# Pool memsets between the indirect transfers of some side chains in a four-layer kernel

## The chip, the cores and the metric

The kernel runs on one core of a Trainium2 chip. The metric is the device time of one execution in microseconds, as the median of several executions without the profiler. Besides these, one execution was taken by the hardware profiler; all durations of single instructions come from it.

## What is computed

Four layers follow each other on x of 4 x 1024 tokens with 128 features, all in float32. Each layer is an attention-like part and a feed-forward part, each added to x and followed by a layer norm:

```python
x = L0_attn_x                                                # (4, 1024, 128)
x = _layernorm(x + _L0_attn_ref(x, ...), axis=-1)            # scans along the tokens
x = _layernorm(x + _L0_ffn_ref(x, ...), axis=-1)             # quantised product
x = _layernorm(x + _L1_attn_ref(x, ...), axis=-1)            # complex linear recurrence
x = _layernorm(x + _L1_ffn_ref(x, ...), axis=-1)             # 16 experts, 4 per token, and a shared one
x = _layernorm(x + _L2_attn_ref(x, ...), axis=-1)            # causal softmax attention, 16 heads of 8
x = _layernorm(x + _L2_ffn_ref(x, ...), axis=-1)             # 8 experts, 2 per token
x = _layernorm(x + _L3_attn_ref(x, ...), axis=-1)            # gated Toeplitz mix over the batch rows
x = _layernorm(x + _L3_ffn_ref(x, ...), axis=-1)             # 32 experts, 4 per token, and a shared one
```

The feed-forward parts of layers 1 to 3 are what matters here. In each, a router gives every token its k best experts and their weights. The token's output is the weighted sum of what these experts make of it, for instance in layer 3:

```python
topk_scores, topk_idx = jax.lax.top_k(softmax(flat @ router_w.T + router_bias), 4)
h = silu(einsum('nd,ehd->neh', flat, gate_w)) * einsum('nd,ehd->neh', flat, up_w)
expert_out = einsum('neh,edh->ned', h, down_w)
out = (take_along_axis(expert_out, topk_idx[:, :, None], axis=1) * topk_scores[:, :, None]).sum(1)
```

## The kernel before

**Tiling.** x stays in SBUF as 32 tiles of 128 tokens by 128 features. Tiles are grouped in four quarters of the sequence, and the layers work on parts: in layer 1 part a (quarters 0 and 1) and part r (quarters 2 and 3), in layer 2 a, m and n (m and n are quarters 2 and 3 of two batch rows each), in layer 3 a, b and c (b and c are one quarter each).

**The expert stage, as five steps.** A route function (l1_route, l2_route, l3_route, each ending in positions) runs mostly on DVE. It computes for every token and choice a row in a list sorted by expert: the tiles pos, for instance posl1r for layer 1, part r, written at L1276. spread (L1313) scatters the tiles of x into that list in DRAM (l1rr, l2ra, l2rm, l2rn, l3ra, l3rb, l3rc), with one indirect transfer for each tile and choice, 128 rows of 512 bytes. The experts function (small_experts for layers 1 and 3, l2_experts for layer 2) loads the list in groups of 512 rows (xg) and computes each tile with its expert's weights. Each such load waits for all transfers of the list. It writes the result to another list (l1yr, l2ya, ...). collect (L1381) gathers the rows of each tile back (yt), again with one indirect transfer for each tile and choice, and DVE adds them, weighted, to x (L1392). Then the tiles are normed and the next layer begins.

All indirect transfers go through one helper, indirect (L1299, the transfer itself at L1301), on Pool's queue. The helper also ties every transfer behind the two before it, so that they stay in the order of the program.

**The order of the work.** The functions are generators. Each yields an estimate, in microseconds, of what the step just emitted will take. run drains a generator; mix(main, side) emits the main generator's steps, and after each as many of the side generator's steps as the estimates allow (pace is a factor on the side's), so that the side's instructions stand between the main's on PE, ACT, DVE and Pool. queued adds that a side instruction stands behind the last main one of its engine. With drain, the rest of the side comes after the main; press drains the side until a condition holds. served lets a chain be served together with others that begin once a condition holds, and chain and abreast put generators one behind the other or side by side. One indirect transfer is entered as 1.26 us, at three places: spread and collect yield 1.26 times the choices, and indirect adds 1.26 to moved_by, the date by which Pool is thought to have issued all so far. collect adds a tile's rows no earlier than moved_by + 4.0 in planned time.

**The stages that the change touches**, in the order of the method all:

| main stage | side beside it |
|---|---|
| l2_attn(0): layer 2 attention, quarters 0 and 1 | l1_route(r), spread of l1rr |
| l1_experts(r), l1_shared(r) | loads of wall2, l2_route(a), spread of l2ra |
| l2_experts(a2) | l1_close(r): collect of l1yr, norm, transposes |
| l2_attn(1): layer 2 attention, quarters 2 and 3 | collect of l2ya, l3_attn(a), l3_route(a), spread of l3ra; once enough rows are done, route and spread of l2rm and l2rn |
| l2_experts(m2), l2_experts(n2) | the rest of these; collect of l2ym |
| l3_shared(a), l3_experts(a) | collect of l2yn, l3_attn(b), l3_route(b) |
| l3_shared(b), l3_experts(b), then the same for c | spread of l3rb and l3rc, collect of part a and b, l3_attn(c), l3_route(c) |

l3_shared(b) and (c) put their result in a tile of its own, which DVE adds to x (L1962) when the scatter of that part has read x.

Of the kernel before, what the change touches and what calls it, by code (L numbers as in the profile page):

```python
# [20 lines left out]
P = 128  # L21
B, L, D = 4, 1024, 128
# [18 lines left out]
E1, F1, NG1, TKG1, K1 = 16, 128, 4, 2, 4  # L41
# [2 lines left out]
FS3 = 512  # L44

H3, D13 = 8, 256

RND = 12582912.0
PI_IN = 3.1415925
# [25 lines left out]
class Kernel:  # L75
    def __init__(self, ctx, tc, ins, out, cols, consts, rows):
        self.tc, self.nc, self.ins, self.out = tc, tc.nc, ins, out
        self.count = itertools.count()
        nc = self.nc
        self.const = self.pool(ctx, "const")  # L80
        self.small = self.pool(ctx, "small", 3)
        self.routes = self.pool(ctx, "routes")
        self.side = self.pool(ctx, "side", 2, space=PSUM)
        dram = self.pool(ctx, "dram", space=DRAM)

        self.cols_t = self.load(self.const, ins["cols"])
        self.cst_t = self.load(self.const, ins["consts"])
        self.x = self.tile(self.const, [P, NT, D], "x")
        self.xT = self.tile(self.const, [P, NT * P], "xT")
        nrow = ins["rows"].shape[1]  # L90
        self.rows_t = self.tile(self.const, [P, nrow], "rows")
        nc.gpsimd.dma_start(out=self.rows_t, in_=ins["rows"].to_broadcast([P, nrow]))
        self.col = {k: self.cols_t[:, a:b] for k, (a, b) in cols.items()}
        self.cst = {k: self.cst_t[:, a:b] for k, (a, b) in consts.items()}
        self.row = {k: self.rows_t[:, a:b] for k, (a, b) in rows.items()}
        self.ident = self.cst["ident"]
        self.eps = self.tile(self.const, [P, 1], "eps")
        nc.vector.memset(self.eps, LN_EPS)
        self.halfpi = self.tile(self.const, [P, 1], "halfpi")
        nc.vector.memset(self.halfpi, math.pi / 2)  # L100
        self.ones = self.tile(self.const, [P, E3], "ones")
        nc.vector.memset(self.ones, 1.0)
        self.rnd = self.tile(self.const, [P, 1], "rnd")
        nc.vector.memset(self.rnd, RND)
        self.zero = self.tile(self.const, [P, D], "zero")
        nc.gpsimd.memset(self.zero, 0.0)
        self.flag = self.tile(self.const, [1, 1], "flag", I32)
        self.hm = self.tile(self.const, [P, 4], "hmg")

        self.first, self.rest = Part("a", 0, 2), (Part("b", 2, 1), Part("c", 3, 1))  # L110
        self.parts = (self.first, *self.rest)
        self.by_rows = (
            Part("a", 0, 2, range(B), 0), Part("m", 2, 2, (0, 1), NT // 2), Part("n", 2, 2, (2, 3), 3 * NT // 4)
        )

        self.rows_done = 0

        self.listed = set()

        self.traced, self.latest = nc.cur_bb.bb.instructions, {}  # L120
        self.now = self.moved_by = 0.0
        self.moved = []

        self.lists, self.route = {}, {}
        self.both = (self.first, Part("r", 2, 2))
        for lay, ne, k in (("l1", E1, K1), ("l2", E2, K2), ("l3", E3, K3)):
            for pt in {"l1": self.both, "l2": self.by_rows, "l3": self.parts}[lay]:
                tl = -(-((pt.nt * P * k + (P - 1) * ne) // P) // 4) * 4
                self.lists[lay, pt.name] = (
                    self.tile(dram, [tl * P, D], f"{lay}r{pt.name}"), self.tile(dram, [tl * P, D], f"{lay}y{pt.name}"), tl  # L130
                )
        self.wall2 = self.tile(dram, [P, E2 * 3 * F2], "wall2")
        self.xsave = self.tile(dram, [P, NT, D], "xsave")

        self.ksave = self.tile(dram, [P, B, BLK], "ksave")
        self.vsave = self.tile(dram, [P, B, 4, (NH + 1) * VW], "vsave")
# [1162 lines left out]
    def indirect(self, apart=(), **kw):  # L1299

        ins = self.nc.gpsimd.indirect_dma_start(**kw)  # L1301

        for o in apart:
            self.tc.declare_no_dep(ins.ins, o.ins.name, reason="rows differ")
        behind = mybir.DependencyInfo(mybir.DependencyClass.NoSync, mybir.DependencyReason.DATA)
        mine = [o.ins.name for o in apart]
        for o in [o for o in self.moved if o not in mine][-2:]:
            self.tc.add_manual_dep(ins.ins, o, behind, reason="queued behind")
        self.moved = self.moved[-130:] + [ins.ins.name]
        self.moved_by = max(self.moved_by, self.now) + 1.26  # L1310
        return ins

    def spread(self, lay, part, k):  # L1313

        pos, _, _, done, _ = self.route[lay + part.name]
        rows = self.lists[lay, part.name][0]
        for t in range(part.nt):
            for i in range(k):
                ins = self.indirect(
                    apart=done,  # L1320
                    out=rows, out_offset=bass.IndirectOffsetOnAxis(ap=pos[:, t, i : i + 1], axis=0),
                    in_=self.x[:, part.order[t], :], in_offset=None,
                )
                done.append(ins)
            yield (1.26 * k,)
        self.listed.add(lay + part.name)

    def gathered(self, pool, rows, g, done, want):
# [52 lines left out]
    def collect(self, lay, part, k, yp, first=0, nt=None, which=None):  # L1381

        nc = self.nc
        pos, wk = self.route[lay + part.name][:2]
        assert f"made {lay}{part.name}" in self.listed
        ys = self.lists[lay, part.name][1]
        late = []

        def add():
            t, yt, _ = late.pop(0)  # L1390
            for i in range(k):
                nc.vector.scalar_tensor_tensor(  # L1392
                    self.x[:, part.order[t], :], yt[:, i, :], wk[:, t, i : i + 1], self.x[:, part.order[t], :],
                    ALU.mult, ALU.add,
                )

        for t in which or range(first, first + (nt or part.nt)):
            yt = self.tile(yp, [P, k, D], "yt")
            for i in range(k):
                self.indirect(  # L1400
                    out=yt[:, i, :], out_offset=None, in_=ys,
                    in_offset=bass.IndirectOffsetOnAxis(ap=pos[:, t, i : i + 1], axis=0),
                )

            late.append((t, yt, self.moved_by + 4.0))
            if len(late) == yp.bufs:
                while late[0][2] > self.now:
                    yield (1.0,)
                add()
            yield (1.26 * k,)  # L1410
        while late:
            while late[0][2] > self.now:
                yield (1.0,)
            add()
            yield (0.36 * k,)
# [471 lines left out]
    def all(self):  # L1887
        a, rest = self.first, self.rest
        b, c = rest
        r = self.both[1]  # L1890
        a2, m2, n2 = self.by_rows
        with ExitStack() as ctx:
            lgp = self.pool(ctx, "l2lg")
            self.l2_lg = self.tile(lgp, [P, NT, E2], "lg")
            with ExitStack() as early:
# [13 lines left out]
                with ExitStack() as c2:  # L1909
                    wall = self.l1_wall(c2)  # L1910
# [3 lines left out]
                    self.run(self.mix(self.abreast(self.l2_weights(), side), self.l1_close(a, yp)))  # L1914
            with ExitStack() as c2:
                wall = self.l1_wall(c2)
                self.run(self.mix(self.l2_attn(0), self.chain(self.l1_route(r), self.spread("l1", r, K1))))
                wall2, loads = self.l2_wall(c2, True)
                yp = self.pool(c2, "l1yr", 5, right=True)
                self.run(self.mix(self.chain(self.l1_experts(r, wall), self.l1_shared(r)), self.chain(loads, self.routed(a2))))  # L1920
                self.run(self.mix(self.l2_experts(a2, wall2), self.l1_close(r, yp)))
            listed = lambda name: lambda: name in self.listed
            on = self.served(
                self.chain(self.rows_in(a2), self.onward(a, True)),
                (lambda: self.rows_done >= B + 2, self.routed(m2)),
                (lambda: self.rows_done == 2 * B, self.routed(n2)),
            )
            self.run(self.mix(self.l2_attn(1), on, drain=False))
            with ExitStack() as c3:
                with ExitStack() as c2:  # L1930
                    wall = self.l2_wall(c2)
                    self.press(on, listed("l2m"))
                    self.run(self.mix(self.l2_experts(m2, wall), on, drain=False))
                    self.press(on, lambda: {"l2n", "routed l3a"} <= self.listed)
                    sw, wall3 = self.l3_wall(c3, True)
                    on = self.chain(on, self.rows_in(m2))
                    self.run(self.mix(self.l2_experts(n2, wall), on, drain=False))
                self.press(on, listed("l3a"))
                yp = self.pool(c3, "l3y", 8)
# [207 lines left out]
```

## Time and profile before

| what | value |
|---|---|
| median of 3 executions without the profiler | 2050.22 us (2046.76 to 2051.03) |
| the profiled execution | 2413.21 us |
| its span, first to last instruction | 2411.4 us |
| mean granted clock of TensorE in it | 0.818 |
| PE busy (matmul) | 1616.9 us, 67% of the span |
| DVE busy | 1263.6 us, 52% |
| ACT busy | 825.0 us, 34% |
| Pool busy | 722.6 us, 30%, of which nearly all indirect transfers |

The profiled execution took 363 us longer than the median of the others. A group in the profile is one line of the code with its operation and tiles; it is given with its count, its busy time, the mean duration of one in nanoseconds, and the time for which its engine sat idle just before, with what ended that. PE is the matmul, PEld the load of its weights. "issue" stands for idle time in which the engine waited for nothing that the profile shows, "remote" for a wait whose end the profile can't put down to an instruction. For Pool's indirect transfers the busy time is that on Pool; the data land later.

The streams of transfers that the change touches, in the profiled execution:

| stream | transfers | first start to last end, us |
|---|---|---|
| l1rr | 64 | 703.3 to 784.2 |
| l2ra | 32 | 957.5 to 997.8 |
| yt from l1yr | 64 | 1024.3 to 1182.7 |
| yt from l2ya | 32 | 1214.7 to 1294.0 |
| l2rm | 16 | 1488.7 to 1508.7 |
| l2rn | 16 | 1653.1 to 1673.0 |
| l3ra | 64 | 1722.5 to 1810.7 |
| yt from l2ym | 16 | 1811.0 to 1830.8 |

### The profile page before, as it was taken

What the parts mean: (1) busy time and instruction counts of PE and PEld (TensorE: products, weight loads), DVE (VectorE), ACT (ScalarE), POOL (GpSimd) and SP (SyncE); (2) the same over time, 40 slices, a digit from 0 to 9 for tenths busy, and PEclk for the clock granted to TensorE, in tenths of its full rate; (3) what the DMA queues carried; (4) which work ended last, traced back from release to release, by engine and by line L of the source; (5) the groups of instructions that cost most, each with busy time, mean ns of one, the idle gap of its engine ahead of it and who ended that gap; (6) DMA issues with size and microseconds to landing.
All of it is one profiled execution on the core that took longest, in us unless ns stands there. A gap on an engine that the chain in (4) does not pass through costs nothing. (4 is left out here: it accounts for less than half of the span.)

```text
span 2411.4 us, 27036 instructions
## 1 busy us (share of the span) xinstructions
PE 1616.9 (67%) x9017; PEld 967.3 (40%) x9017; DVE 1263.6 (52%) x3630; ACT 825.0 (34%) x1180; POOL 722.6 (30%) x681
## 2 busy tenths in 40 slices
PE   7626876975661778487969787887745798357160
PEld 3214333853320337345623232344523486245160
DVE  8957894655570565224545675473611265236233
ACT  6701571422330333122236564642201164223030
POOL 1031484135227000435132002002272200735725
PEclk9856887988785888788979998988977899678575
DMA  9930002334101016212130000031321131222232
GB/s 309 288 112 0 20 34 90 112 115 160 62 31 53 15 34 200 83 44 74 38 106 21 1 1 16 3 114 40 143 85 35 44 112 46 76 79 62 89 89 68
DMA packets 215530, 187.10 MB, mean 78 GB/s; under 512 B 16528, under 2 KB 194064, under 8 KB 214864
## 3 DMA queue, kind: packets, MB, share of 16 engines
q1 hardware_dynamic: 194672, 142.29, 18.7%
q0 software_dynamic: 20704, 42.86, 5.8%
q8 instruction: 84, 1.38, 0.2%
q14 instruction: 70, 0.57, 0.1%
HBM read 88.49 MB, written 96.60 MB: 77 GB/s over the span
## 5 line engine op out<-in xcount | busy, mean ns | idle before, releaser
L1055 ACT ACTIVATE pr<-sc 128x1024 f32<-128x1024 f32 x288 | 279.7, 1021 | 319.9 <-PE sc L157 184.9
L157 PE MATMUL gu<-ld,xgT 128*128 x640 | 177.4, 423 | 88.8 <-issue 38.7
L157 PE MATMUL sc<-qm,kT 32*128 32x512 f32 (+3 forms) x1536 | 199.2, 558 | 13.7 <-issue 12.3
L157 PE MATMUL s<-pr,va 128*32 128x512 f32 (+3 forms) x1536 | 177.1, 528 | 46.0 <-issue 26.2
L157 PEld LDWEIGHTS gu<-ld,xgT 128*128 128x128 f32 x640 | 127.5, 210 | 119.1 <-issue 49.7
L165 PE MATMUL tp<-ld,hg 128*128 128x128 f32 x624 | 104.0, 289 | 92.1 <-ACT hT L167 38.0
L169 DVE COPY hT<-tp 128x512 f32<-128x512 f32 x118 | 81.0, 686 | 159.3 <-remote 73.9
L157 PE MATMUL gu<-wall,xgT 128*128 x304 | 156.1, 640 | 2.7 <-ACT xgT L167 2.0
L1061 DVE TENSOR_TENSOR pr<-pr,ld 128x512 f32<-128x512 f32 (+1 forms) x160 | 92.2, 581 | 100.6 <-ACT pr L1055 98.5
L165 PEld LDWEIGHTS tp<-ld,hg 128*128 128x128 f32 x624 | 81.5, 149 | 144.7 <-issue 46.9
L165 PE MATMUL tp<-ld,xg 128*128 128x128 f32 x396 | 68.9, 305 | 102.1 <-DMA xg<-l3rc 48.5
L1749 DVE TENSOR_TENSOR hg<-sg,gu 128x256 f32<-128x256 f32 x160 | 65.8, 417 | 134.9 <-ACT sg L1748 95.8
L167 ACT COPY xgT<-tp 128x512 f32<-128x512 f32 x99 | 58.0, 586 | 213.0 <-PE tp L165 91.1
L157 PEld LDWEIGHTS sc<-qm,kT 32*128 32x128 f32 x1536 | 84.8, 197 | 113.6 <-issue 77.4
L1507 ACT ACTIVATE sg<-gu 128x512 f32<-128x512 f32 x76 | 45.2, 597 | 225.7 <-PE gu L157 109.4
L1748 ACT ACTIVATE sg<-gu 128x256 f32<-128x256 f32 x160 | 61.1, 385 | 163.2 <-PE gu L157 80.9
L1301 POOL DMA_INDIRECT l1ra<-x,posl1a x64 | 93.1, 1455 | 59.5 <-DVE posl1a L1276 40.3
L157 PEld LDWEIGHTS s<-pr,va 128*32 128x32 f32 x1536 | 38.9, 113 | 156.6 <-issue 109.5
L1509 DVE TENSOR_TENSOR hg<-sg,gu 128x512 f32<-128x512 f32 x76 | 51.7, 682 | 92.1 <-ACT sg L1507 48.7
L1301 POOL DMA_INDIRECT yt<-l1yr,posl1r x64 | 60.9, 951 | 124.1 <-DVE x L1392 79.3
L165 PEld LDWEIGHTS tp<-ld,xg 128*128 128x128 f32 x396 | 52.4, 158 | 107.6 <-issue 59.0
L1301 POOL DMA_INDIRECT l1rr<-x,posl1r x64 | 61.7, 965 | 99.5 <-DVE posl1r L1276 80.3
(440 smaller groups left out, 3498.8 us busy)
## 6 DMA issues: line engine op xcount, KB each, us to landing
wall<-wall SPq DMA_DIRECT2D x16, 768.0 KB
l3ra<-zero SPq DMA_DIRECT2D x1, 6144.0 KB
ld<-in_l_w SPq DMA_DIRECT2D x2, 3072.0 KB
wall<-we SPq DMA_DIRECT2D x24, 256.0 KB
ld<-in_l_w SPq DMA_DIRECT2D x1, 6144.0 KB
l1ra<-zero SPq DMA_DIRECT2D x1, 5120.0 KB
l1rr<-zero SPq DMA_DIRECT2D x1, 5120.0 KB
xg<-l3ra SPq DMA_DIRECT2D x20, 256.0 KB
```

What stands on the lines that cost most here:

```text
L157: return self.nc.tensor.matmul(out, lhsT, rhs, start=start, stop=stop)
L165: nc.tensor.transpose(pt[:, k * P : (k + 1) * P], s, self.ident)
L167: nc.scalar.copy(dst, pt[:, : n * P])
L169: nc.vector.tensor_copy(dst, pt[:, : n * P])
L1055: nc.scalar.activation(pr, sc[h], AF.Exp)
L1061: nc.vector.tensor_tensor(d, d, cst["tril"].unsqueeze(1).unsqueeze(1).to_broadcast([P, 2, n, P]), ALU.mult)
L1301: ins = self.nc.gpsimd.indirect_dma_start(**kw)
L1507: nc.scalar.activation(sg, gu[:, 0, :], AF.Silu)
L1509: nc.vector.tensor_tensor(h, sg, gu[:, 1, :], ALU.mult)
L1748: nc.scalar.activation(sg, pg[:, :, 0, :], AF.Silu)
L1749: nc.vector.tensor_tensor(h[:, 2 * c : 2 * c + 2, :], sg, pg[:, :, 1, :], ALU.mult)
```

## The change

A new tile idle of 384 columns is only ever written. While a generator is wrapped in spaced, every indirect transfer that it issues is followed on Pool by a memset of 384 (LONG) or 256 (SHORT) columns of that tile, tied behind it. The estimate of one transfer becomes 1.26 us plus 0.0009 us for each column, at the three places that had 1.26. Eight streams are wrapped, the ones of the table above, with SHORT for l3ra and l2ym and LONG for the others. The remaining streams (part a of layer 1, l2yn, and all of layer 3 but l3ra) are as they were.

```diff
+LONG, SHORT = 384, 256
...
+        self.idle = self.tile(self.const, [P, LONG], "idle")
+        self.rest_cols = 0
...
         self.moved = self.moved[-130:] + [ins.ins.name]
-        self.moved_by = max(self.moved_by, self.now) + 1.26
+        if self.rest_cols:
+            stay = self.nc.gpsimd.memset(self.idle[:, : self.rest_cols], 0.0)
+            self.tc.add_manual_dep(stay.ins, ins.ins.name, behind, reason="queued behind")
+            self.moved.append(stay.ins.name)
+        self.moved_by = max(self.moved_by, self.now) + self.step
         return ins
+
+    @property
+    def step(self):
+        return 1.26 + self.rest_cols * 0.0009
+
+    def spaced(self, gen, cols=LONG):
+
+        while True:
+            self.rest_cols = cols
+            got = next(gen, None)
+            self.rest_cols = 0
+            if got is None:
+                return
+            yield got
...
-            yield (1.26 * k,)
+            yield (self.step * k,)
...
-                self.run(self.mix(self.l2_attn(0), self.chain(self.l1_route(r), self.spread("l1", r, K1))))
+                self.run(self.mix(self.l2_attn(0), self.chain(self.l1_route(r), self.spaced(self.spread("l1", r, K1)))))
...
-                self.run(self.mix(self.chain(self.l1_experts(r, wall), self.l1_shared(r)), self.chain(loads, self.routed(a2))))
-                self.run(self.mix(self.l2_experts(a2, wall2), self.l1_close(r, yp)))
+                self.run(self.mix(self.chain(self.l1_experts(r, wall), self.l1_shared(r)), self.chain(loads, self.spaced(self.routed(a2)))))
+                self.run(self.mix(self.l2_experts(a2, wall2), self.spaced(self.l1_close(r, yp))))
...
-                self.chain(self.rows_in(a2), self.onward(a, True)),
-                (lambda: self.rows_done >= B + 2, self.routed(m2)),
-                (lambda: self.rows_done == 2 * B, self.routed(n2)),
+                self.chain(self.spaced(self.rows_in(a2)), self.spaced(self.onward(a, True), SHORT)),
+                (lambda: self.rows_done >= B + 2, self.spaced(self.routed(m2))),
+                (lambda: self.rows_done == 2 * B, self.spaced(self.routed(n2))),
...
-                    on = self.chain(on, self.rows_in(m2))
+                    on = self.chain(on, self.spaced(self.rows_in(m2), SHORT))
```

More of the change, by code (lines that the diff above doesn't have):

```diff
@@ L1409, in collect @@
                 add()
-            yield (1.26 * k,)
+            yield (self.step * k,)
         while late:
```

## The prediction

> **What bounds the kernel now.** I read the page first, then the Pool's groups, then the stretches around each stream of indirect transfers. A stream here is a run of such transfers one behind the other.
>
> ```profile
> span 2411.4 us, 27036 instructions
> ...
> POOL 1031484135227000435132002002272200735725
> ```
>
> The second line is Pool's busy share in 40 slices of 60.3 us: it is no bound, but is full during its streams. Their price, and that of a memset:
>
> ```profile
> L1301 POOL DMA_INDIRECT l1ra<-x,posl1a x64 | 93.1, 1455 | 59.5 <-DVE posl1a L1276 40.3 <-issue 19.2
> ...
> L1301 POOL DMA_INDIRECT l1rr<-x,posl1r x64 | 61.7, 965 | 99.5 <-DVE posl1r L1276 80.3 <-issue 19.2
> ...
> L340 POOL MEMSET keep<- 128x1024 f32 x1 | 1.0, 952 | 0.0
> ...
> L106 POOL MEMSET zero<- 128x128 f32 x1 | 0.2, 232 | 0.0
> ```
>
> Columns: busy us, mean ns of one | idle us before. A transfer holds Pool 0.965 us and is followed by 0.30 us of "issue" (19.2/64): one per 1.265 us. Now what the other engines do beside the 64 transfers of l1rr (703.3 to 784.2 us), columns PE, PEld, DVE, ACT, POOL busy, then PE's clock, DMA share, GB/s:
>
> ```profile
> 632.00:719.00 87.00, 66.68 (x488) 31.68 (x487) 61.68 (x226) 34.51 (x36) 12.09 (x13) 0.87 0.08 30
> 719.00:793.00 74.00, 8.95 (x21) 2.39 (x20) 2.05 (x6) 1.38 (x2) 49.66 (x52) 0.50 0.12 47
> 793.00:900.00 107.00, 87.80 (x763) 43.82 (x763) 68.00 (x175) 45.61 (x47) 0.00 (x0) 0.90 0.05 19
> ```
>
> From 16 us into the stream until 9 us after it, the attention stands still. At the end of the l3ra and l2ym streams (1722 to 1831 us), PE and then ACT:
>
> ```profile
> 1796.29 2.72 PE L157 MATMUL gu<-wall,xgT 128*128 x4
> 1836.97 1.11 PE L165 MATMUL tp<-ld,hg 128*128 128x128 f32 x4 [37.95 <-ACT hT L167]
> ```
>
> ```profile
> 1826.53 0.60 ACT L1507 ACTIVATE sg<-gu 128x512 f32<-128x512 f32 x1 [42.80 <-remote]
> ```
>
> PE's product ends at 1799.0, and ACT, which needs only that, is released at 1826.5: PE's signal is 27.5 us late. I went through every wait of ACT and DVE (over 0.3 us) on PE's semaphore and compared its end with PE's last matmul end before it. With at most 7 indirect transfers begun in the 20 us before: 629 waits, those over 1 us late sum to 4.3 us. With 8 or more: 177 waits, 498 us. Laid on one time line (two engines often wait together), all late stretches cover 250 us, of which 170 beside streams that the change spaces.
>
> So the question is whether executions without the profiler have this hold-up. I think not, for three reasons. The profiled execution took 2413.2 us, 363 more than the median of 2050.2; taking out the 250 us, and 34 us in which PE stutters between two of them (734 to 768), leaves 2129, still above the median. Signals are prompt for the first 10 to 15 us of a stream, and then stop, sooner where PE issues many instructions; the stream beside the light PE work at 505 to 527 us shows at most 3 us. [...] And it is not instructions that are missing: the instruction queue fetched 16 KB in 1.1 us at 743.3, mid-stream.
>
> What bounds the unrecorded kernel is then its stages in turn: PE (67% of the span, 113 of 130 us in the second half of l2_attn(1)) and the hand-over between side chains and stages, as where DVE adds the shared part (columns: us, times, longest):
>
> ```profile
> DVE x L1962 <- DMA l3rc<-x,posl3c: 33.7, 1, 33.7
> ```
>
> [...]
>
> **The change part by part.**
>
> *Memsets.* 224 of 384 columns (64 l1rr, 32 l2ra, 64 l1yr, 32 l2ya, 16 l2rm, 16 l2rn) and 80 of 256 (64 l3ra, 16 l2ym). From the two rows: (952 − 232)/896 = 0.80 ns a column, so 232 + 256 × 0.80 = 437 ns and 335 ns. Pool gets 224 × 0.437 + 80 × 0.335 = 125 us more. Least: they vanish in the 0.30 us of issue but for 0.14 us, 31 + 3 = 34 us; most: each brings an issue of 0.30 of its own, 216 us. I take 1.70 us a transfer (LONG) and 1.60 (SHORT), the earliest memsets on the page standing with no idle time before them. Each waits only for the memset before it on the same engine, so only transfers queue behind it.
>
> *l1rr:* 64 × 0.437 = +28 us: ends at 812. l2_attn(0), which ends at 900, would end at 826 without the 74 us: hidden, 14 us left. At the upper price it ends at 832, 6 us on the path. *l2ra:* +14 us on an end at 86 us after the experts' start at 911; experts and l1_shared last 155, or 124 less hold-up: hidden. *l1yr:* Pool starts 20 transfers before the stage and sits idle 79.3 us of it for DVE's adds (its group's idle time by releaser, x L1392): hidden by that. *l2ya, l2rm, l2rn:* +14, +7, +7 beside l2_attn(1) and l2_experts(m2), whose lists are ready early: hidden; l2rn has the least cover.
>
> *The planner.* The step grows from 1.26 to 1.61 and 1.49, so side work is placed later among PE's, DVE's and ACT's instructions. Built, both kernels have the same instructions on these engines, and the same order on DVE until the first add of l1yr. Three moves stand on the path:
> 1. The norm closing l1_close(r) (L209, 2.1 us, ahead of the last expert tiles now, 1205 us) goes behind the first instructions of l2_attn(1), which needs its transposes: its 2.1 us plus transposes and copies, +4 us (0 to 8).
> 2. l3ra and l2ym: 64 × 0.335 + 16 × 0.335 = +27 us on Pool, and the planner knows 0.23 of the 0.335. Without hold-up, l2ym would be gathered at about 1811 to 1831, ahead of its adds (L1392, after the second block of l3_shared). Afterwards 1836 to 1862, while the adds move by about one block of 10.5 us (1901.6 to 1912.0): DVE waits, with the products of l3_shared behind it and PE behind these. +7 us (0 to 14).
> 3. That lateness shifts l3_attn(b) and l3_route(b). topk and weigh of b (2019.7 to 2024.5, 4.9 us) now lie before the first product of l3_shared(b); afterwards behind four, and the positions behind eight. posl3b comes at 2046.1; I take +7 us (3 to 12). The scatter l3rb follows it with nothing beside it from 2066 to 2089, so this is paid in full.
>
> Of moved steps, each takes its DMAs along: the load of xg waits for all of its list, and SP's other loads queue behind that wait, covered as above. [...]
>
> **Sum:** 4 + 7 + 7 + 2 = +20 us on 2050.2: **2070 us**. Durations come from the profiled execution, whose own sum is another: 2413 + 20 less what spacing frees of the 170 to 204 us of hold-up, about 2250, with the median not following. Main case's own range: 2055 (lower ends, 3 us and more) to 2105 (8 + 14 + 12 + 5 + 6 for l1rr, and as much again unseen).
>
> **The rivals.**
> - *The hold-up is real* and exists unrecorded (the other side). Place: PE's signals beside long streams; price: up to 204 us; it decides as soon as more than 20/204, a tenth, of it remains in plain executions. For it: it begins at a rate, with no hold-up at up to 7 transfers in 20 us, and l1ra at 1.76 us a transfer passes freely (PE 88.8 of 126 us); spacing makes 1.70. Against it: the 363 us. At a third: 2050 + 20 − 68 = 2002 us.
> - *All is hidden*: the waits in 2 and 3 are covered by side work that had slack anyway: 2050 ± 4. For it: l3_attn(b) has the whole of l3_experts(a) to catch up in; against it: scatter l3rb is exposed.
> - *The memset does not space* (it lies within the 0.30 us): only the planner acts: 4 + 7 + 2 = 2063. It belongs with the main case.
>
> **How the numbers follow.** Within 0.2% (4 us) is about what a measurement can tell from no change. Main case with the last rival 0.55, hidden 0.12, real hold-up 0.33: slower 0.55, same 0.12, faster 0.33. The range reaches to the real hold-up at two fifths (2050 + 20 − 82 = 1988) and up to 2105; outside lie about 0.1 below and 0.07 above.
>
> **What would show it.** Step by step in the profile after: transfers 1.70 and 1.60 us apart; l1rr ending before l2_attn(0); a later gap before x L1962 at l3b; waits of DVE at L1392 for l2ym. The late PE signals shrink in the recorded span, by far more than the median does. I am wrong if the median falls with the span.

## The result and the profile after

The change makes the kernel slower: 2104.05 us (2099.95 to 2106.48, 4 runs) against 2050.62 us (2046.76 to 2052.37, 4 runs) beside it, a ratio of 1.0261 with a 95% interval of 1.0239 to 1.0283. That is 53 us more, where 20 were forecast.

The profiled execution of the changed kernel took 2104.62 us, as long as its other executions. The one of the kernel before, from which the prediction was made, had taken 2413.21 us, 363 more than its median. So a difference of these two traces isn't the effect of the change. On the page of after, the line of Pool and the groups that answer to those shown of before are these:

```profile
span 2102.8 us, 27331 instructions
...
POOL 2013078304630880587344000402268700665755
...
L1315 POOL MEMSET idle<- 128x384 f32 (+1 forms) x304 | 124.7, 410 | 0.2
...
L1305 POOL DMA_INDIRECT l1rr<-x,posl1r x64 | 65.1, 1017 | 93.1 <-DVE posl1r L1280 82.5
```

The memsets cost what was worked out (410 ns in the mean; by form 439 ns for 384 columns and 329 ns for 256). But they don't lengthen each transfer by that much: the idle time behind a transfer of l1rr falls from 0.30 us to (93.1 − 82.5)/64 = 0.17 us. Part of a memset lies where Pool waited anyway.

A later run of the kernel before (e12 below) has a trace of an execution as fast as the others: 2049.42 us, beside a median of 2051.87. Its page:

```profile
span 2047.6 us, 27036 instructions
...
POOL 2012168403650570274332000300347600755755
```

**Where the time went.** The next two fences give stretches of this trace and of the trace after, cut at the same points of the program: from DVE's first work for l2_experts(a2), to its last for it, to its last for l2_attn(1), to its last for the experts of m2 and n2, to its first for l3_experts(a). Columns: stretch, length, busy us (count) of PE, PEld, DVE, ACT and Pool, then PE's clock, DMA share and GB/s. First the kernel before (e12), then the changed kernel:

```profile
916.00:1031.00 115.00, 113.60 (x618) 77.66 (x616) 70.97 (x182) 43.15 (x72) 45.30 (x48) 1.00 0.23 70
1031.00:1404.00 373.00, 316.73 (x2391) 123.62 (x2392) 233.96 (x713) 212.83 (x225) 47.57 (x48) 0.94 0.10 33
1404.00:1565.00 161.00, 148.81 (x739) 101.26 (x738) 88.66 (x284) 44.22 (x75) 60.47 (x63) 0.91 0.32 116
1565.00:1620.00 55.00, 47.09 (x205) 29.44 (x206) 17.92 (x36) 10.89 (x19) 41.87 (x44) 0.95 0.26 82
```

```profile
924.00:1052.00 128.00, 116.22 (x611) 78.54 (x609) 69.85 (x172) 39.40 (x67) 79.69 (x116) 0.96 0.23 64
1052.00:1422.00 370.00, 314.92 (x2371) 119.72 (x2372) 223.62 (x672) 215.59 (x229) 67.82 (x96) 0.94 0.09 32
1422.00:1586.00 164.00, 149.51 (x767) 102.06 (x765) 98.86 (x335) 46.89 (x77) 63.90 (x95) 0.93 0.32 114
1586.00:1665.00 79.00, 49.05 (x204) 30.68 (x205) 17.38 (x34) 10.72 (x18) 68.92 (x104) 0.80 0.20 63
```

Two stretches grow, with PE's work in them nearly unchanged: the experts of a2 by 13 us, l3_shared(a) by 24 us. Together with what lies ahead and behind, this is the lateness at each point, in us (times in the trace; the middle column is a run with the memsets alone, e13 below):

| point | before (e12) | memsets alone (e13) | change |
|---|---|---|---|
| Pool's first transfer of l1rr | 678.1 | +2.2 | +7.1 |
| DVE's last of l2_attn(0) | 795.7 | +9.2 | +11.7 |
| DVE's first of l2_experts(a2) | 915.6 | +5.6 | +8.2 |
| ACT's first exponential of l2_attn(1) | 1052.9 | +7.1 | +17.1 |
| DVE's last of l2_attn(1) | 1404.4 | +8.9 | +17.5 |
| DVE's last of the experts of m2 and n2 | 1564.6 | +8.3 | +21.3 |
| DVE's first of l3_experts(a) | 1620.2 | +19.4 | +45.4 |
| DVE's first of l3_experts(b) | 1788.6 | +19.4 | +54.5 |
| end | 2047.6 | +23.4 | +55.2 |

Up to the first transfer of l1rr no memset has run, and PE, DVE and ACT have the same instructions in the same order in all three traces. So the 2.2 and 7.1 us at that point belong to the executions compared, not to the change, and differences of this size between traces of different comparisons can't be read as its effect. In the run with memsets alone the order on these three engines is that of the kernel before to the end.

The waits name the two places. DVE's waits for gathered rows (columns: us, times, longest) in the kernel before (e12), and then in the changed one:

```profile
DVE x L1392 <- DMA yt<-l2ym,posl2m: 5.3, 3, 2.3
```

```profile
DVE x L1414 <- DMA yt<-l2ym,posl2m: 28.6, 2, 27.8
...
DVE x L1414 <- DMA yt<-l1yr,posl1r: 19.2, 8, 9.4
```

At x L1414 (L1392 before) DVE adds the rows of l2ym. It came 27.8 us too early, and PE sat behind it: 49 us of work in 79 us. For l1yr there were no waits at this line before; now 19.2 us, within l2_experts(a2).

**The late signals of PE.** In e12 they aren't there: over 347 waits of DVE and ACT for PE with 8 or more transfers in the 20 us before, the lateness over 1 us sums to 4.6 us, where the trace of 2413 us had 498 over 177. The comparisons below come in two kinds, by the chip on which they ran: the kernel before takes about 2050 us in all its executions (2042.90 to 2062.02), or about 2400 us in all (2387.73 to 2419.24). Only runs beside 2050 us are of the kind in which the change was measured.

### The profile page after: what moved, and what is told of

The parts are those of the page before. It is cut to its first block, busy times and chain, and to the rows that moved or that the text cites. A ratio compares the mean times of both kernels' runs of the same rounds, so it can differ in the third digit from the quotient of the medians.

```text
span 2102.8 us, 27331 instructions
## 1 busy us (share of the span) xinstructions
PE 1547.9 (74%) x9017; PEld 938.8 (45%) x9017; DVE 1265.4 (60%) x3630; ACT 826.6 (39%) x1181; POOL 850.0 (40%) x985
## 5 line engine op out<-in xcount | busy, mean ns | idle before, releaser
L161 PE MATMUL sc<-qm,kT 32*128 32x512 f32 (+3 forms) x1536 | 189.5, 545 | 1.0 <-ACT pr L1059 1.0
L161 PE MATMUL gu<-ld,xgT 128*128 x640 | 169.8, 410 | 23.1 <-DVE hg L1771 20.5
L161 PE MATMUL s<-pr,va 128*32 128x512 f32 (+3 forms) x1536 | 164.2, 523 | 19.2 <-DVE pr L1065 7.7
L161 PE MATMUL gu<-wall,xgT 128*128 x304 | 148.1, 611 | 6.6 <-ACT xgT L171 3.8
L169 PE MATMUL tp<-ld,xg 128*128 128x128 f32 x396 | 65.9, 295 | 88.1 <-DMA xg<-l3rc 49.6
L1315 POOL MEMSET idle<- 128x384 f32 (+1 forms) x304 | 124.7, 410 | 0.2
L1305 POOL DMA_INDIRECT l1ra<-x,posl1a x64 | 93.1, 1454 | 59.3 <-DVE posl1a L1280 40.1
L173 DVE COPY hT<-tp 128x512 f32<-128x512 f32 x118 | 80.7, 684 | 58.4 <-PE tp L169 58.3
L1305 POOL DMA_INDIRECT l1rr<-x,posl1r x64 | 65.1, 1017 | 93.1 <-DVE posl1r L1280 82.5
L169 PE MATMUL tp<-ld,hg 128*128 128x128 f32 x624 | 97.5, 277 | 5.4 <-DVE hg L1771 2.7
L1305 POOL DMA_INDIRECT l2rm<-x,posl2m x16 | 16.1, 1008 | 190.3 <-DVE posl2m L1280 187.8
L1305 POOL DMA_INDIRECT l3ra<-x,posl3a x64 | 63.2, 988 | 66.1 <-DVE posl3a L1280 51.6
```

The lines of the kernel that those rows point to most:

```text
L161: return self.nc.tensor.matmul(out, lhsT, rhs, start=start, stop=stop)
L169: nc.tensor.transpose(pt[:, k * P : (k + 1) * P], s, self.ident)
L173: nc.vector.tensor_copy(dst, pt[:, : n * P])
L1315: stay = self.nc.gpsimd.memset(self.idle[:, : self.rest_cols], 0.0)
```

## The experiments

### The first comparison, beside 2399 us

**e1** is the kernel before, without an edit. 

> The kernel before, unchanged, with a new profile. If PE's late signals are an artefact of one recorded execution, the new profile need not have them: its own time would then lie at 2046 to 2055 us, and shows where the 53 us of the change come from, stage by stage. If they belong to the kernel whenever it is recorded, the profile takes about 2413 us again. If they belong to the kernel as such, no execution is possible at 2050 us without them, and the new profile at 2050 us must show late signals of some tens of us.

It took 2395.95 us, beside 2399.15 us; the profiled execution 2402.8 us. The late signals are in it, in the same places and of the same size (473 us over 172 waits). The reading "an accident of one recorded execution" falls. DVE and ACT wait for releases that the profile can't place:

```profile
ACT pr L1055 <- remote: 117.3, 6, 69.7
ACT sg L1507 <- remote: 65.7, 4, 42.1
DVE hT L169 <- remote: 65.4, 7, 19.0
DVE t L169 <- remote: 62.5, 1, 62.5
```

"remote" waits sum to 538 us here (46 of them, counting groups of 4.8 us and more), and in e12, of the same program, there are none down to groups of 2.5 us. Landings of transfers are fewer on record too: 7951 in this trace, 15601 in that of e12.

**e2**, the planner's step without the memsets:

```diff
-            stay = self.nc.gpsimd.memset(self.idle[:, : self.rest_cols], 0.0)
-            self.tc.add_manual_dep(stay.ins, ins.ins.name, behind, reason="queued behind")
-            self.moved.append(stay.ins.name)
```

> The planner's step of 1.26 + 0.0009 us a column stays, but no memset is emitted: the order of the change with transfers as close as before. Theory (the transfers of l3ra and l2ym end later than the adds that need them): without memsets the gather of l2ym ends 27 us earlier, its wait at the adds goes, and what is left is the norm of l1_close behind the first instructions of l2_attn(1) and the later routing of part b: 2055 to 2070 us. Rival (the order alone costs it): 2095 to 2110 us. Rival (it is only Pool's length): 2046 to 2054 us.

**e3**, the memsets without the planner's step:

```diff
-        return 1.26 + self.rest_cols * 0.0009
+        return 1.26
```

> All 304 memsets are emitted, but the planner's step stays 1.26 us, so the order on PE, DVE and ACT is that of the kernel before (but for steps that wait for the true date). Theory: the gather of l2ym is as late as with the change, and the adds stand where they stood before, so DVE waits for them as long or longer: 2085 to 2110 us, with 25 to 40 us of waiting at the first add of l2ym's rows. Rival (the order alone costs it): 2046 to 2056 us.

**e4**, neither memsets nor step for l3ra and l2ym:

```diff
-                self.chain(self.spaced(self.rows_in(a2)), self.spaced(self.onward(a, True), SHORT)),
+                self.chain(self.spaced(self.rows_in(a2)), self.onward(a, True)),
...
-                    on = self.chain(on, self.spaced(self.rows_in(m2), SHORT))
+                    on = self.chain(on, self.rows_in(m2))
```

> Only the LONG streams are spaced; l3ra and l2ym go as in the kernel before. Theory: the 27.8 us wait of DVE for l2ym's rows goes, and with it the lateness of everything behind it; what is left is the norm of l1_close (4 us, 0 to 8), [...] and whatever the later routing of part b costs: 2052 to 2066 us. Rival (the long spacings cost it, in l2_attn(0) to l2_attn(1)): 2085 to 2105 us.

Measured: e2 2409.24 us, e3 2151.57, e4 2236.83, all beside 2399.15. None of the three fits its expectation, since these were made for a kernel before of 2050 us. The comparison tells something else. In this comparison the time falls with the number of streams that are spaced: e2, which spaces none, stays 10 us above the kernel before, e4, which leaves out l3ra and l2ym, is 162 us below it, and e3, which spaces all eight, 248. In e3 almost no late signal lies beside the streams that it spaces (of its 121 us, 100 lie beside the two gathers of l3ya and l3yb, which it doesn't space). And e3 is faster than the change itself turns out to be here (e5), though both have the same memsets: a first sign that the planner's part costs.

In the traces of e1 and e2 the order can be read, though not the time: l3ra begins 107 us after DVE's last of l2_attn(1) in e1 and 129 us after it in e2, 22 us later with no memset anywhere.

**e5** is the changed kernel, without an edit. 

> The changed kernel, unchanged. In the last comparison the kernel before took 2399 us in every execution, with PE's late signals in its trace, where it had taken 2050 us in the comparison of the change. Theory (late signals are a condition of the chip or of its recording, and spacing takes them away): the changed kernel takes 2095 to 2115 us whatever the kernel before takes beside it, 2050 or 2399 us. Rival (the changed kernel gets slower too under that condition): 2200 us or more beside 2399 us.

It took 2184.32 us beside 2397.67 us: a ratio of 0.9108 (0.9078 to 0.9137). So the change is 9% faster on such a chip and 2.6% slower on the other kind. Theory and rival both miss, and the rival by less: the changed kernel gets slower too, by 80 us. Late signals remain beside the streams that it leaves alone, above all those of layer 3 (late stretches of 99 us in all, with 20 us of DVE's wait for l2ym among them).

**e6** spaces every stream:

```diff
-        self.rest_cols = 0
+        self.rest_cols = LONG
...
-            self.rest_cols = 0
+            self.rest_cols = LONG
             if got is None:
```

> Every stream of indirect transfers is spaced by 384 columns, those of layer 1 part a, l2yn and layer 3 too. Theory (late signals of PE come only with dense streams): none is left in the trace, so the time is the same whether the kernel before takes 2050 or 2399 us beside it: 2104 us plus what the added memsets cost where the stream is waited for, 0.437 us for each of the 32 transfers of l3rb, of l3rc and of the last gather, 42 us, and up to 30 us for the others: 2145 to 2180 us. Rival (late signals come from the volume of records, not their density): with 2399 us for the kernel before, 2220 us or more.

2175.42 us, beside 2407.2: within the theory's range. Hardly a late signal is left: over 371 waits with 8 or more transfers before them the lateness sums to 32 us, and the longest, 15 us, lies at l3_shared(a), where DVE waits for l2ym. Yet landings are missing here too (12271 on record). So signals aren't late wherever records are missing; in these traces they are late where records are missing and the transfers follow each other closely (those of l1rr are 1.26 us apart in e1, with 473 us of lateness in the whole trace, and 1.62 us in e6, with 32).

### The quiet base, beside 2054.6 us

To be free of the chip, all four kernels of this comparison have memsets of 256 columns also behind the transfers that the change leaves alone, not entered with the planner (e7):

```diff
+LONG, SHORT, OTHER = 384, 256, 256
+TOLD = {384: 384, 256: 256}
...
-            self.rest_cols = cols
+            self.rest_cols, self.told = cols, TOLD[cols] if tell else 0
             got = next(gen, None)
-            self.rest_cols = 0
+            self.rest_cols, self.told = OTHER, 0
...
-        return 1.26 + self.rest_cols * 0.0009
+        return 1.26 + self.told * 0.0009
```

> The changed kernel, with 256-column memsets also behind the transfers that the change leaves alone (those are not entered with the planner), so that no stream is dense enough for late PE signals: a common base for the three runs beside it. Expected 2120 to 2155 us: 2104 us, and 0.19 us for each of the 96 transfers of l3rb, l3rc and the last gather, 18 us, and up to 30 us for the others.

**e8** has the same memsets, and the step back at 1.26 (`return 1.26`). 

> All memsets of e7, but the planner's step is 1.26 us everywhere, so the order on PE, DVE and ACT is that of the kernel before. Theory (the longer step pushes DVE's routing of layer 3 part a back by the planned time of the streams before it, 64 x 0.35 = 22 us, and what needs posl3a with it): 15 to 30 us under e7, l3ra begins 15 to 26 us sooner after the end of the second half of layer 2's attention, and DVE's wait for l2ym's rows falls from about 28 to under 12 us. Rival (the memsets' own time on Pool is the whole cost): within 6 us of e7.

**e9** leaves only three chains untold:

```diff
-                self.chain(self.spaced(self.rows_in(a2)), self.spaced(self.onward(a, True), SHORT)),
-                (lambda: self.rows_done >= B + 2, self.spaced(self.routed(m2))),
-                (lambda: self.rows_done == 2 * B, self.spaced(self.routed(n2))),
+                self.chain(self.spaced(self.rows_in(a2), tell=False), self.spaced(self.onward(a, True), SHORT)),
+                (lambda: self.rows_done >= B + 2, self.spaced(self.routed(m2), tell=False)),
+                (lambda: self.rows_done == 2 * B, self.spaced(self.routed(n2), tell=False)),
```

> e7, but the planner isn't told of the memsets of three chains alone: the gather of l2ya and the scatters l2rm and l2rn, which stand beside the second half of layer 2's attention ahead of the routing of layer 3 part a. Theory: these 64 entries of 0.35 us are what pushes l3_route(a) back; l3ra begins 15 to 26 us sooner than in e7, and the time is 10 to 25 us under e7. Rival (the norm of l1_close pushed into the attention, or the entries of l3ra and l2ym, cost it): within 5 us of e7.

**e11** is e8 with the memsets behind l3ra and l2ym doubled:

```diff
+            self.times = 2 if cols == SHORT else 1
...
+            for _ in range(self.times):
                 stay = self.nc.gpsimd.memset(self.idle[:, : self.rest_cols], 0.0)
```

> e8 with two memsets of 256 columns instead of one behind each of the 80 transfers of l3ra and l2ym: about 0.33 x 80 = 26 us more of Pool in that chain. Theory (that chain has little slack left in the old order, 10 us of waiting in the run with memsets alone): 15 to 27 us over e8. Rival (the chain is covered by l3_shared and the experts of n2): within 5 us of e8.

| run | us | against | DVE's wait for l2ym, us (longest) | l3ra begins after DVE's last of l2_attn(1), us |
|---|---|---|---|---|
| e7 change | 2131.38 | | 28.3 (27.7) | 113.6 |
| e8 old order | 2093.86 | e7 − 37.5 | 16.6 (13.2) | 90.9 |
| e9 three chains untold | 2110.5 | e7 − 20.9 | 13.4 (12.8) | 93.9 |
| e11 old order, twice the short ones | 2118.73 | e8 + 24.9 | 40.4 (34.0) | 94.0 |

This comparison fell beside 2054.6 us. The order alone is worth 37.5 us, 20.9 of them in the three chains: telling the planner of 64 transfers more by 384 × 0.0009 = 0.35 us each, 22 us, puts l3_route(a) behind them 20 us later, though it runs on DVE and isn't waiting for them: it needs nothing of the 32 scatters, and the rows of the 32 gathers of l2ya have all been fetched 380 us before it starts (1131.6 and 1512.0 us in the trace after). The rival of e8 and e9 falls. In e8 the wait for l2ym is 16.6 us, over the 12 that were expected: the memsets alone leave one. e11 says why: its l3ra takes 119.3 us instead of 99.4 and its l2ym 29.5 instead of 23.0, 26.4 us more on Pool, and 24.9 of these arrive in the time. That chain has no slack in this order. DVE's waits for l2ym in e9, and in e11:

```profile
DVE x L1415 <- DMA yt<-l2ym,posl2m: 13.4, 2, 12.8
```

```profile
DVE x L1419 <- DMA yt<-l2ym,posl2m: 40.4, 5, 34.0
```

### Before and memsets alone, beside 2053.4 us

**e12** is the kernel before once more, for its trace. 

> The kernel before, unchanged, once more with a profile, because comparisons differ in whether it takes 2050 or 2400 us. Theory (late signals of PE come only where the records of semaphores are also lost, a condition of the chip): if it takes about 2050 us here, the profile shows no signal of PE more than 4 us late, all landings of transfers are on record, l3ra takes 81 to 88 us, and DVE waits under 10 us for l2ym's rows; if about 2400 us, late signals and lost records come together again. Rival (late signals are there at 2050 us too): some tens of us of them at 2050 us.

**e13** is e3 once more. 

> All 304 memsets with the order of the kernel before, beside it. Theory, where the kernel before takes 2050 us: the order is 25 to 40 us of the change's 53 us, so memsets alone give 2064 to 2080 us, with a wait of 10 to 18 us for l2ym's rows. Rival (Pool's length alone): 2095 to 2110 us. Where the kernel before takes 2400 us: about 2150 us as in the run before.

e12 took 2051.87 us, with 15601 landings on record and no signal of PE over 4.6 us late. l3ra took 88.7 us, l2ym's waits 5.3 us. The theory holds: in seven comparisons on six chips, the kernel before took 2400 us exactly where landings were missing from the traces of that comparison, and 2050 us where they were on record. e13 took 2072.31 us, a ratio of 1.0089 (1.0055 to 1.0123): 18.9 us, 11 to 25. So the memsets are 19 us of the change, and the planner's order, on top of the memsets, the other 34 (32 by the two spans, 2102.8 − 2071.0; 37.5 in the quiet base). In e13, DVE's wait is

```profile
DVE x L1414 <- DMA yt<-l2ym,posl2m: 14.6, 3, 11.1
```

where e12 has 5.3 and the change 28.6.

### Two more comparisons, beside 2408 us

These are on the division of the order's part; both ran on chips with late signals.

**e14** and **e18** are e2 once more. 

> The order of the change without a memset, beside a kernel before of about 2050 us (the run before this one was made beside 2399 us). Theory (the later places cost even when Pool is as fast as before, since the routing of layer 3 part a is late by order; the waits for l1yr's and l2ym's rows shrink by what Pool is faster): 2068 to 2088 us, with l3ra beginning 17 to 22 us later after the end of the attention's second half than in the kernel before. Rival (order and memsets cost only together): 2050 to 2060 us.

> The order of the change without a memset. Beside a kernel before of about 2050 us, theory (l3_route(a) and what follows it is late by order, even with Pool as fast as before): 2068 to 2088 us. Rival (order and memsets cost only together): 2050 to 2060 us. Beside 2400 us: about 2410 to 2420 us, and nothing new.

2420.14 us (ratio 1.0048, 1.0022 to 1.0073) and 2415.07 us (1.0037, 1.0020 to 1.0054). With e2's, these are three comparisons in which the order alone costs 6 to 12 us beside 2400 us. Whether it costs its 34 us without memsets at 2050 us stays open. What the traces do show is its place: l3ra begins 129 us after DVE's last of l2_attn(1) in all three, against 107 in e1 and 113.4 with the change.

**e15** and **e19** are the change with l1_close untold:

```diff
-                self.run(self.mix(self.l2_experts(a2, wall2), self.spaced(self.l1_close(r, yp))))
+                self.run(self.mix(self.l2_experts(a2, wall2), self.spaced(self.l1_close(r, yp), tell=False)))
```

> The change, but the planner isn't told of the memsets in l1_close. Theory (its 64 entries of 0.35 us put the last adds and the norm of l1yr behind; the stage from the first instruction of l2_experts(a2) to the first of l2_attn(1) on ACT takes 134 us instead of 112): this stage is 112 to 116 us again, DVE's 19 us of waits for l1yr go, and the time is 6 to 14 us under the change: 2090 to 2098 us. Rival (the stage's lateness is made up in the attention that follows): 2101 us or more.

> The change with l1_close not entered with the planner. Beside a kernel before of about 2050 us, theory (10 us of the change's cost are the adds and the norm of l1yr, put behind): 2090 to 2098 us, 53 less 6 to 14 us over the kernel before. Rival (made up in the attention that follows): 2101 us or more. Beside 2400 us: about 2177 us again.

2177.41 us (0.9041, 0.9004 to 0.9077) and 2181.93 us (0.9054, 0.9015 to 0.9094), where the change itself had 0.9108 (0.9078 to 0.9137) in another comparison: the intervals overlap or nearly touch, so the time proves nothing. The stages do: from l2_experts(a2) to the end of l2_attn(1), e5 takes as long as the change does without late signals (146 us to the first exponential, 498 in all; below). The 112 and 134 us of the expectation end at the load of ACT's table for the exponentials, which starts 25 us before the first of them in the kernel before (e12) and 12 in the change, so they overstate the move (e15 has 112 again, e5 133). From DVE's first of l2_experts(a2) to ACT's first exponential of l2_attn(1) it is 133 us in e15 and 134 in e19, 146 in e5 and in the change, 137 in the kernel before; to DVE's last of l2_attn(1) it is 485 us in e15 and e19, 498 in e5 and in the change, 489 in the kernel before. DVE's waits for l1yr go from 19.5 us to none. So telling the planner of l1_close costs 12 to 13 us up to that point.

**e16** has the long memsets alone, in the old order (e4 with `return 1.26`). 

> The 224 memsets of 384 columns alone, with the order of the kernel before and none behind l3ra and l2ym. Theory (of the 19 us that all memsets cost in the old order, 11 are l3ra and l2ym ending 15 us later and 8 are the long ones): 2058 to 2066 us, l3_shared(a) waits under 7 us for l2ym's rows. Rival (the long ones are hidden): 2050 to 2055 us.

2220.38 us beside 2407.73; late signals fill l3_shared(a) from 1597 to 1636 us of its trace, so it doesn't tell the long memsets' cost.

**e17** is the kernel before with three chains entered as shorter than they are:

```diff
+LESS = -400
...
-                self.chain(self.rows_in(a2), self.onward(a, True)),
-                (lambda: self.rows_done >= B + 2, self.routed(m2)),
-                (lambda: self.rows_done == 2 * B, self.routed(n2)),
+                self.chain(self.spaced(self.rows_in(a2)), self.onward(a, True)),
+                (lambda: self.rows_done >= B + 2, self.spaced(self.routed(m2))),
+                (lambda: self.rows_done == 2 * B, self.spaced(self.routed(n2))),
```

> The kernel before without any memset, but the gather of l2ya and the scatters l2rm and l2rn are entered as 0.90 us a transfer instead of 1.26. Theory (the place of l3_route(a) follows the planned time of the chains ahead of it): posl3a and with it l3ra come 10 to 23 us sooner after the attention's end; what follows is then bound by PE in l3_shared(a) and by the exposed scatters of parts b and c, so the time falls by 0 to 10 us: 2042 to 2054 us. Rival (sooner routing takes DVE's time from the attention and costs more): 2056 us or more.

2427.87 us (1.0089, 1.0056 to 1.0122). l3ra begins 70 us after DVE's last of l2_attn(1) instead of 107, so the place follows the planned time in this direction too; it moved 37 us for the 23 entered less, more than forecast. Among late signals the time can't be read for the other kind of chip. None of the kernels that were run beside 2050 us beats the one before. Where the kernel before takes 2400 us, e3 is the fastest of those tried, and at 2050 us (as e13) it loses 0.9% instead of the change's 2.6%.

## Why the prediction was right in direction and wrong in size

The forecast was +20 us, measured is +53. Its terms, by its own steps:

- **The late signals aren't the change's business in its own comparison: right.** The median didn't follow the span. That the hold-up belongs to the recorded execution is only in part shown: late signals and missing records went together on all six chips wherever transfers were dense (473 us with 7951 landings on record in e1, 4.6 us with 15601 in e12), and what ties the two no run shows. Every execution on these chips has its span on record, so how they run with nothing recorded is open. The 363 us aren't what the full profile adds to an execution, as the prediction had it: in e1 the profiled execution took 2402.8 us and the others 2387.73 to 2406.09. The rival of a real hold-up describes those chips, where its upper price came in: 213 us less (e5), against up to 204. How soon a stream's signals turn late can be put in numbers in the trace before: work of PE whose signal is over 1 us late first ends 8.5 us into the scatter l2rm, where PE begins 16 instructions a us, 8.8 into l2ra (12), 12.2 into l2rn (10), 16.0 into l1rr (9.5) and 16.3 into l3ra (7).
- **The memsets' price: right per instruction, too dear per stream.** 329 and 439 ns against 335 and 437. Taken were 1.70 and 1.60 us a transfer; measured are 49.6/32 = 1.55 us for l2ra (863.8 to 913.4), and 98.4/64 = 1.54 us for l3ra (1535.3 to 1633.7), which took 88.7/64 = 1.39 us before. So Pool's chain of l3ra and l2ym grew by 9.7 + 2.9 = 12.6 us, not 27.
- **l1rr hidden: the cover held, and little of the cost beside it lasts.** l1rr ends 19 us before l2_attn(0) does. That stage ends 9.2 us later with memsets alone and 11.7 with the change, but 2.2 and 7.1 of these were there at l1rr's first transfer; the stage itself adds 7.0 and 4.6, and at l2_experts(a2) 3.4 and 1.1 of it are left. The sum's 2 us (0 to 5), for DVE's work beside the memsets in all stages, were the author's estimate, with no trace behind it. Two groups of DVE take longer beside them, in like stretches around l1rr, in the kernel before (e12) and after:

```profile
L938 DVE TENSOR_SCALAR qm<-qT,hmg 128x512 f32<-128x512 f32 x8 | 3.4, 483 | 0.1
...
L209 DVE TENSOR_SCALAR x<-x,mv,rstd 128x128 f32<-128x128 f32 x12 | 3.3, 354 | 0.1
```

```profile
L942 DVE TENSOR_SCALAR qm<-qT,hmg 128x512 f32<-128x512 f32 x8 | 5.5, 743 | 0.1
...
L213 DVE TENSOR_SCALAR x<-x,mv,rstd 128x128 f32<-128x128 f32 x12 | 4.0, 515 | 0.1
```

  These are operations of the type TENSOR_SCALAR with one input from SBUF: 743 ns instead of 483, 515 instead of 354. Within the changed kernel's l2_attn(0) alone, those of qm that overlap a memset take 835 ns in the mean, the others 478. The products with two inputs (pr, 128x512) take 687 ns before and 686 after. It is 2.1 + 0.7 = 2.8 us of DVE in this stage; the rest isn't tied to a group. The transfers of l1ra, which no memset follows, vary with what DVE does beside them as well: of the 64 in the trace before (1455 ns in the mean), the 22 that lie mostly beside its scans take 2016 ns, and the 5 that lie mostly beside TENSOR_SCALAR 976.
- **Move 1, the norm of l1_close: right in kind, +4 forecast, about +9 measured.** ACT's first exponential of l2_attn(1) comes 146 us after the start of l2_experts(a2) instead of 137. The first of them, before (e12) and after (columns: start, us; in brackets ACT's idle time before it):

```profile
1052.92 1.94 ACT L1055 ACTIVATE pr<-sc 128x1024 f32<-128x1024 f32 x2 [23.93 <-PE sc L157]
```

```profile
1070.03 1.94 ACT L1059 ACTIVATE pr<-sc 128x1024 f32<-128x1024 f32 x2 [10.88 <-PE sc L161]
```

  Not the norm's own 2.1 us moved but the last adds of l1yr: their last is 125 us after that start instead of 104, behind 19 us of DVE's waits. The prediction had called l1yr hidden by Pool's idle 79 us. Pool was; the date at which the planner allows the adds was not, and it had grown by 64 × 0.35 = 22 us. l2_attn(1) gives none of it back: the lateness goes from +8.2 to +17.1 at the first exponential and +17.5 at its end. With l1_close untold it goes away (e15, e19).
- **Move 2, l3ra and l2ym: the step that failed.** "+7 us (0 to 14)" became 24: the stretch of l3_shared(a) grew from 55 to 79 us. The prediction let l2ym's gather slip by Pool's 27 us, let the adds move by 10.5, behind one more block of l3_shared, and had no term for a later start of l3ra after the attention. In fact l2ym's gather ends at 1657.1 instead of 1607.4, 49.7 us later: 17.5 by what is late already, 19.4 since l3ra begins 113.4 instead of 94.0 us after the attention's end, and 12.6 by the memsets. The adds didn't move: the first stands behind the second block in both traces, and follows the first transfer of l2ym by 2.5 us. So what it waits for is the end of l3ra, which comes 19.4 + 9.7 = 29 us later, counted from the attention's end; 4 of these pass in the experts of m2 and n2, the rest is waiting. The 19.4 are the term that wasn't in the sum; of the terms that were, the memsets' 27 was twice too large, and the 10.5 of the adds should have been nothing. "Three moves stand on the path", it said; the fourth is l3_route(a), put behind 22 us of planned time that stands for work of Pool's queue alone. The start of the stream in both traces, before (e12) and after:

```profile
L1301 POOL DMA_INDIRECT l3ra<-x,posl3a x64: 954/958/1337, 1498.4 to 1586.2; - x64
```

```profile
L1305 POOL DMA_INDIRECT l3ra<-x,posl3a x64: 963/964/1422, 1535.3 to 1632.7; - x64
```

  The prediction could not see that this chain has no slack, as its trace had it under late signals: there the rows of l2ym lay ready 70 us before their adds. In e12 DVE already waits 5.3 us for them.
- **Move 3, the routing of part b: right.** +7 (3 to 12) forecast; l3_experts(b) begins 54.5 us late after 45.4 at part a, so +9, and +10 to the end. The places are those forecast: topk of b starts 5 us ahead of the first product of l3_shared(b) in e12 and 10 us after it in the changed kernel, behind four products, with the positions behind eight; l3rb begins 30 us after that product instead of 22. With memsets alone this step adds nothing (+19.4 at both parts).
- **Sum.** By the points of the trace: 8 (to the experts of a2, 7 of them ahead of the first memset) + 9 (to the end of the attention) + 4 (experts of m2 and n2) + 24 (l3_shared(a)) + 9 (to l3_experts(b)) + 1 = 55, against 4 + 7 + 7 + 2. The range's upper end, 2105, doesn't come out of its terms: 8 + 14 + 12 + 5 + 6 = 45 give 2095, and 2101 with the last counted twice.

Left open: the order without memsets at 2050 us, how much of the 12 to 13 us that l1_close costs up to the attention's end (e15, e19) arrives in the time, and what makes a chip lose records.

## What to carry to other kernels

When one estimate serves both as the price of a transfer on its queue and as the time that a planner lets pass for a chain, raising it delays work on other engines that isn't waiting for the transfers: here 34 of 53 us. Before counting a memset's own time, ask which later step of another engine is placed behind the sum of these estimates, and what slack the chain behind that step has; a second memset behind each transfer measures that slack directly (e11: 24.9 of 26.4 us arrived). And when a profiled execution is a sixth longer than the median of the others (2413 us beside 2050 here), get another trace before pricing stalls or slack from it.

## What the runs showed of the hardware that was not expected

- Six chips ran the same program in two ways, each in all executions: medians of 2053 to 2055 us with 15,601 landings on record (e12), or 2398 to 2409 us with 7,951 (e1). In the second kind, PE's signals come up to 39 us late beside dense indirect transfers (e1), and spacing every stream takes nearly all of it away: 473 us in sum in e1, 32 in e6, where 64 transfers of l1rr take 103.5 us instead of 80.7 and those of l3ra 99.4 instead of 87.6.
- A memset of 256 or 384 columns behind an indirect transfer lengthens the pace by 0.15 us (l3ra) and 0.30 us (l2ra: 40.1 us before, 49.6 after, for 32) for its 0.33 and 0.44 us of work.
- Beside Pool's memsets, two groups of DVE's TENSOR_SCALAR on SBUF take 54 and 45% longer in the mean (483 to 743 ns, 354 to 515), those of the first that overlap a memset 835 ns; products of two inputs (686 ns) stay as they were.
